# An earlier chain of end columns, earlier border loads, and a split of the weights without masks

## The chip, the core and the metric

The kernel runs on one core of a Trainium2 chip. The core has a matrix engine (PE, with its weight loads shown apart as PEld), a vector engine (DVE), a scalar engine (ACT), a general engine (POOL) and a queue that issues DMA transfers (SP). Each engine takes its instructions in the order of its own queue and waits on semaphores for the others. The metric is the device time of one execution in microseconds (us); for a kernel it is the median of its runs.

## The reference

The program adds two blocks to x, an array of 32 samples by 64 channels by 1024 positions. Each block is a chain of four modulated convolutions followed by a feed-forward part over the 1024 positions as features:

```python
x = x + _L0_ffn_ref(_L0_cond_ref(x, cond_512, ...), L0_ffn_A, L0_ffn_B, L0_ffn_Wr)
x = x + _L1_ffn_ref(_L1_cond_ref(x, cond_512, ...), qweight, scales, zeros, bias)

# _L0_cond_ref and _L1_cond_ref: 4 layers, 'same', 'upsample', 'same', 'downsample'
s = style @ mw.T + mb                          # a scale for each sample and channel
weight = SCALE * w * s[:, None, :, None]       # 64 x 64 x 3 for each sample
weight = weight * rsqrt(sum(weight * weight))  # normalised over input channel and tap
out = conv(x, weight) + b                      # up- and downsampling with a blur (1, 3, 3, 1)

# _L0_ffn_ref: 64 experts of rank 16, the best 16 for each of the 2048 rows
scores = xf @ Wr.T
top_vals, top_idx = top_k(scores, 16)
gates = softmax(top_vals)                      # scattered into G, 2048 x 64
h = einsum('nd,krd->nkr', xf, A)
out = einsum('nkr,kdr->nd', h * G[:, :, None], B) * 2

# _L1_ffn_ref: weights of 4 bits, unpacked
W = scales * q - zeros
out = x @ W + bias
```

All of it is in 32-bit floats. The kernel works on 16 pairs of samples, two samples of 64 channels on the 128 partitions.

## The kernel before

**Stages.** For the first block the kernel goes through the 16 pairs, and for each pair p it does the following, with the parts of neighbouring pairs laced into one another. `begin` prepares the positions. `first` (c, L760 and L761, for later pairs L772 and L777) is the first part of the four convolutions. `composed1` and `composed2` (`compose` and `weights` in the main loop) multiply the last layers' weights of the pair into one another: g at L600, f at L623, the evictions of f by ACT at L638, L640 and L641, and sums by POOL at L646 and L652. `rest` (`later` in the main loop, r at L811 for the first samples, at L838, L856 and L879 for others) is the rest of the convolutions with the composed weights, which leaves the tokens thx of the pair. `layer0` multiplies the tokens with A and Wr (h at L959), picks the gates (L993 to L1003, on DVE), and `gated` (L1009, on POOL) multiplies the gates in; the result goes to memory as hgd. When all pairs are done, the kernel turns h round (ht, L1085), multiplies with B (o, L959 again, in `layer0b`) and adds the residual (L1129 and L1130, on DVE), which gives x1. The second block follows in the same manner, with the unpacked weights (q, L1211).

**Whole and split products.** Pairs 0 and 1 use A and B as they came from memory, in full float (araw and, for part 7 of A, kept; braw, which lies in cv). The other pairs use weights taken apart into a high part, a low part and a crossed part in a shorter float format (fp32r): wa for A, wb for B, each in eight parts k. `split_weights` (L375 to L390) makes them. For each part it goes over chunks of 512 columns (A with Wr has 1088 columns, so two chunks of 512 and one of 64; B has 1024). DVE masks the low bits off (L150, into a small buffer wah or wbh), POOL subtracts the masked from the raw weights (L383), and ACT copies the masked into the high part (L384). Over the whole part, DVE then makes the crossed part (L391) from the two. The tokens are split in the same way, by DVE (L150, L923), ACT (L927, L931) and POOL (tdx and tdh, L939). The raw weights of A lie in blocks which later hold split weights: wa5 takes the block of araw0, wa6 that of araw1, and wa7 that of araw2. wb k takes the block of wa k.

**End columns.** The first and last columns of each sample need their own treatment, since the border of each layer is padded. `ends` is a generator that does this for all 16 pairs at once, as a chain: DVE scales the loaded border columns xg of x (L493, L494); PE makes ye (L502), DVE scales it (L474, L477); PE makes ue (L521), DVE scales and blurs it (L530 to L532); PE makes ve (L546), DVE scales and blurs it; PE makes re (L559), DVE adds the bias; PE turns it round (rt, L568), ACT copies it, and DMAs write it to the array red (L574). From there or from rt the outermost rows come to the tokens, for pairs 0 and 1 by the DMAs of `outer` (L907) and for others by those of `outer_outputs` (L590). Each `next(set_ends)` in the main program advances the chain by one step.

**What sets the order.** The program is written once in one order, and each engine gets its own instructions from it in an order that a scheduler makes by priority. `tc.issue_after(x)` holds an instruction behind x, and only an instruction that runs on the same engine as x. The list `beside` gives what is laced in between the stages of a pair's product: `beside[n]` runs ahead of the n-th `next(main)`. Buffers come from pools: h and o use 4 banks of PSUM (fps), f, g, ue, ve and re share one (mps), and ye and c use 3 (cps).

**Loads of the start.** SP issues x of the first pairs, then A and Wr in four groups (`load_a`, L395 to L415: parts 2 to 4, then 5, 0 and 1, then 6, then 7), and then the border columns xg (L413, two transfers of 64 KB).

Of the kernel before, what the change touches and what calls it, by code (L numbers as in the profile page):

```python
# [8 lines left out]
F32 = mybir.dt.float32  # L9
# [3 lines left out]
ALU = mybir.AluOpType  # L13
AX = mybir.AxisListType

P = 128
# [4 lines left out]
NP = B // 2  # L21
L = 1024
# [3 lines left out]
H = 512  # L26
# [12 lines left out]
AW = E + E * R  # L39
# [24 lines left out]
def adaln_ffn_kernel(ctx: ExitStack, tc: tile.TileContext, t, out: bass.AP):  # L64
    nc = tc.nc
# [46 lines left out]
    re = const.tile([P, 2, 2, P], F32, name="re")  # L112
    xg = const.tile([P, NP, 2, 8], F32, name="xg")
# [29 lines left out]
    def block(k, shape, dt, name):  # L143

        return wts.tile(shape, dt, tag=f"w{k}", name=name)

    def high(src, name):

        v = wk.tile([P, H], I32, tag="hi", name=name, bufs=3)[:, : src.shape[1]]
        nc.vector.tensor_scalar(  # L150
            v, src.bitcast(I32), BITS, BITS, ALU.logical_shift_right, ALU.logical_shift_left
        )
        return v.bitcast(F32)

    done, tbl, outers, uppers = {}, {}, {}, {}
    WHOLE = (0, 1)
# [219 lines left out]
    def split_weights(raw, w, ks, into, name, crossed=True):  # L376

        for k in ks:
            ws = block(k, [P, 3, w], F32R, f"{name}{k}")
            for c in range(0, w, H):  # L380
                cs = slice(c, min(c + H, w))
                h = high(raw[k][:, cs], f"{name}h{k}_{c}")
                nc.gpsimd.tensor_tensor(ws[:, 1, cs], raw[k][:, cs], h, ALU.subtract)  # L383
                nc.scalar.copy(ws[:, 0, cs], h)  # L384
            into[k] = ws
            if crossed:
                crossed_weights(into, k)
# [7 lines left out]
    def load_a():  # L395

        wr = t["wrT"].rearrange("(s q) e -> s q e", q=NC)
        av = t["aT"].rearrange("(s q) f -> s q f", q=NC)
        raw = [None] * NC
        for n, parts in enumerate((((2, 5),), ((5, 6), (0, 2)), ((6, 7),), ((7, 8),))):  # L400
            if n < 3:
                r = block(5 + n, [P, 3, AW], F32, f"araw{n}")
            else:
                r = wk.tile([P, AW], F32, tag="w4", name="kept", bufs=3).unsqueeze(1)
            j = 0
            for a, b in parts:
                nc.sync.dma_start(r[:, j : j + b - a, E:], av[:, a:b])
                nc.sync.dma_start(r[:, j : j + b - a, :E], wr[:, a:b])
                for q in range(a, b):
                    raw[q] = r[:, j + q - a]  # L410
                j += b - a
        for s, c in enumerate((0, L - 8)):
            nc.sync.dma_start(xg[:, :, s], t["x"][:, :, c : c + 8].rearrange("n p w -> p n w"))  # L413
        return raw

    def load_b(ks, into):
# [552 lines left out]
    def layer0(p, ws):  # L969

        hs = wk.tile([P, AW], F32, tag="w4", name=f"hs{p}", bufs=3)
        key = f"x0_{p}"
        whole = p in WHOLE

        def joined(col, w, qd):
            dst = hs[:, col : col + w]
            if whole:
                nc.scalar.activation(dst, qd[0], AF.Copy, scale=alp[:, NL - 1, p : p + 1])
                return
            nc.scalar.activation(dst, qd[0], AF.Copy, scale=outd[:, 0, p : p + 1])  # L980
            nc.vector.scalar_tensor_tensor(
                dst, qd[1], outd[:, 1, p : p + 1], dst, ALU.mult, ALU.add
            )

        ga = tiny.tile([P, E], F32, tag="ga", name=f"ga_{p}")

        def gates():
            s0 = hs[:, :E]
            m0 = tiny.tile([P, 8], F32, tag="m0", name=f"m0_{p}")
            m1 = tiny.tile([P, 8], F32, tag="m1", name=f"m1_{p}")  # L990
            s1 = tiny.tile([P, E], F32, tag="s1", name=f"s1_{p}")
            s2 = tiny.tile([P, E], F32, tag="s2", name=f"s2_{p}")
            nc.vector.max(m0, s0)  # L993
            nc.vector.match_replace(s1, m0, s0, LOW)
            nc.vector.max(m1, s1)
            nc.vector.match_replace(s2, m1, s1, LOW)
            su = tiny.tile([P, 1], F32, tag="su", name=f"su_{p}")
            nc.vector.tensor_scalar_mul(su, m0[:, 0:1], -1.0)
            nc.scalar.activation(ga, s0, AF.Exp, bias=su)
            nc.vector.scalar_tensor_tensor(ga, s2, LOW, ga, ALU.is_equal, ALU.mult)  # L1000
            nc.vector.reduce_sum(su, ga, axis=AX.X)
            nc.vector.reciprocal(su, su)  # L1002
            done["gates"] = nc.vector.tensor_scalar_mul(ga, ga, su)  # L1003

        def gated(c):
            a, b = CHUNKS[c]
            v = hs[:, E + a * R : E + b * R].rearrange("p (e r) -> p e r", r=R)
            g = ga[:, a:b].unsqueeze(2).to_broadcast([P, b - a, R])
            nc.gpsimd.tensor_tensor(v, v, g, ALU.mult)  # L1009

        def chunk(c):
            a, b = CHUNKS[c]
            w = (b - a) * R + (E if c == 0 else 0)
            col = a * R + (E if c > 0 else 0)
            banks = [fpst(f"h{p}_{c}_{j}")[:, :w] for j in range(1 if whole else 2)]
            return banks, slice(col, col + w)

        def done_with(c, ch):
            product(ch, key, ws, at, D)
            joined(ch[1].start, ch[1].stop - ch[1].start, ch[0])  # L1020

        if whole:

            three = [chunk(c) for c in range(3)]
            ks = (2, 3, 4, 5, 0, 1, 6, 7)
            for n, k in enumerate(ks):
                for ch in three:
                    product(ch, key, ws, at, Q, (k,), ks[0], ks[-1])
                if n in (0, 1, 2, 3, 5):
                    yield  # L1030
            for c, ch in enumerate(three):
                done_with(c, ch)
            gates()
            yield
            for c in range(3):
                gated(c)
            nc.sync.dma_start(hgd[p], hs[:, E:])
            return

        two = []  # L1040

        ks = tuple(range(6 if p == len(WHOLE) else NC))
        for c in range(2):
            two.append(chunk(c))
            product(two[c], key, ws, at, Q, ks)
            yield
        for c in range(2):
            if p == len(WHOLE):
                product(two[c], key, ws, at, D, ks)
            else:  # L1050
                done_with(c, two[c])
                if c == 0:
                    gates()
            yield
        if p == len(WHOLE):
            for c in range(2):
                product(two[c], key, ws, at, Q, (6, 7))
                product(two[c], key, ws, at, D, (6, 7))
                joined(two[c][1].start, two[c][1].stop - two[c][1].start, two[c][0])
                if c == 0:  # L1060
                    gates()
        ch = chunk(2)
        product(ch, key, ws, at, Q)
        yield
        done_with(2, ch)
        yield
        for c in range(3):
            gated(c)
        nc.sync.dma_start(hgd[p], hs[:, E:])

    def load_h(p):
# [219 lines left out]
    def weights(k):  # L1291
        if k < len(todo):
            fw[k] = composed2(*todo[k], gs.pop(k))

    def later(k, h):
        if k < len(todo):
            i, p = todo[k]
            rest(i, 2 * p + h, ys[k][h], fw[k][h])
# [10 lines left out]
    def split_behind(v, k):  # L1309
        with tc.issue_after(done[v].ins):  # L1310
            split_weights(araw, AW, (k,), wa, "wa")
# [32 lines left out]
    compose(1)  # L1344
    with tc.issue_after(done["c"].ins):
        split_weights(araw, AW, (3,), wa, "wa")
    for h in range(2):
        later(0, h)
    spread_rows(1)
    weights(1)  # L1350
    load(2)
    tables_of(2)
    set_ends = ends(0, 0, NP, block(2, [P, 3 * AW], F32, "room2"))
    next(set_ends)

    for k in range(NP):
# [6 lines left out]
            hg = load_h(0)  # L1363
        main = layer0(k, araw if k in WHOLE else wa)
        next(main)
        if k == 0:
            split_behind("xe", 0)
            split_behind("xe", 1)
        if k + 3 < NP:
            tables_of(k + 3)  # L1370
            if k + 2 >= DIRECT:
                load(k + 3)
        beside = [[] for _ in range(5)]
        if k == 0:
            beside[0] += [(next, set_ends)]
            beside[1] += [(next, set_ends)]
            beside[2] += [(next, set_ends)]
            beside[3] += [(split_behind, "s2", 4), (run, set_ends), (outer, 0), (outer_of, 2)]
            beside[4] += [(split_behind, "re", 2)]
        if not last:  # L1380
            beside[1] += [(later, k + 1, 0)]
            beside[3] += [(later, k + 1, 1)]
# [27 lines left out]
            with tc.issue_after(done["gates"].ins):  # L1410
                split_weights(araw, AW, (7,), wa, "wa", False)
        run(main)
        if k == 0:
            weights(k + 2)
        if not last:
            crossed(f"x0_{k + 1}")

# [3 lines left out]
    for p in range(NP):  # L1421
# [19 lines left out]
        if p == LAST:  # L1441
            load(NP)
            tables_of(NP)
            set_ends = ends(1, 0, LAST, cv[:, O_FW:])
# [108 lines left out]
```

## Time and profile before

| | us |
|---|---|
| median of 3 runs | 893.77 |
| lowest and highest run | 892.96, 894.99 |
| profiled execution | 891.84 |
| its span | 889.8 |
| outside of the span | 2.0 |

| engine | busy us | share of the span |
|---|---|---|
| PE | 861.4 | 97% |
| PEld | 773.3 | 87% |
| DVE | 723.9 | 81% |
| POOL | 531.8 | 60% |
| ACT | 355.6 | 40% |

The profile is of one execution. An instruction's row gives its start from the beginning of the span, its time, its engine and line, what it writes and reads, and, in brackets, how long its engine was idle before it and which instruction of which engine ended this. Rows of like instructions that follow each other are drawn together (x6). PE's granted clock is 1.00 when it is full. The products of the first block run until about 395 us, those with B until about 640, and the second block's after that.

The borders of the stages that the change touches, from the timeline of PE: the first r of pair 0 begins at 29.85, ye is made at 38.53, ue at 41.17, ve at 49.55, re at 54.43 and rt at 59.60. f of pair 2 begins at 72.56. The first r of pair 2 begins at 79.22. The first products with split weights are at 100.93, the last products with A end at 395.5, and the first products with split B begin at 426.53.

### The profile page before, as it was taken

The numbers are of one execution on the slowest core, as the hardware profiler recorded it, in microseconds if no ns is written. First come the engines' busy times: TensorE is split into PE (matmuls) and PEld (weight loads), VectorE is DVE, ScalarE is ACT, GpSimd is POOL, SyncE is SP. The second block draws the span as 40 slices with busy tenths as digits, with TensorE's granted clock in tenths as the row PEclk, the third lists the DMA queues.
The fourth block names the chain that finished last, engine by engine and source line by source line (L and its number), as shares of the span: only waits on it lengthen the run. The fifth ranks groups of instructions, "written<-read, shape, count | busy, mean of one in ns | idle before, by whom it ended". The sixth has DMA issues, their size and how long they took to land.

```text
span 889.8 us, 14891 instructions
## 1 busy us (share of the span) xinstructions
PE 861.4 (97%) x5023; PEld 773.3 (87%) x5023; DVE 723.9 (81%) x1461; ACT 355.6 (40%) x817; POOL 531.8 (60%) x745
## 2 busy tenths in 40 slices
PE   6989989999999999999999999999999999999997
PEld 5877789999999999994688888888899999999996
DVE  5565888888888888768996666669999999999996
ACT  6444444444444444433432221247333433443340
POOL 7335754666666665556572222343887888888884
PEclk9999999999999999999999999999999999999999
DMA  8531213222222222344465765566433234324311
GB/s 244 147 73 51 52 62 86 83 81 82 78 76 74 74 76 72 119 166 155 140 213 193 229 195 175 189 194 190 146 107 110 87 118 118 110 96 140 107 66 72
DMA packets 49739, 107.83 MB, mean 121 GB/s; under 512 B 13764, under 2 KB 22400, under 8 KB 49664
## 3 DMA queue, kind: packets, MB, share of 16 engines
q1 hardware_dynamic: 48704, 105.90, 37.9%
q10 hardware_dynamic: 960, 0.99, 0.5%
q8 instruction: 40, 0.66, 0.3%
q14 instruction: 35, 0.29, 0.1%
HBM read 69.00 MB, written 37.86 MB: 120 GB/s over the span
## 4 chain that ended last, share of the span: by engine, by line
PE 41%; DVE 8%; POOL 2%; issue 2%; ACT 0%; DVEq 0%; POOLq 0%
PE o L959 16%; PE q L1211 11%; PE f L623 3%; PE r L879 2%; PE c L777 2%; PE r L838 1%; PE ht L1085 1%; PE r L847 1%; PE c L772 1%; PE g L600 1%; DVE cv L720 1%; DVE cv L778 1%; DVE r L888 1%; DVE rt L870 1%; DVE nib L443 1%
## 5 line engine op out<-in xcount | busy, mean ns | idle before, releaser
L720 DVE TENSOR_TENSOR cv<-cv 128x257 f32<-128x257 f32 x120 | 106.7, 921 | 1.1 <-ACT cv L762 0.9
L734 POOL TENSOR_TENSOR cv<-cv 128x256 f32<-128x256 f32 x120 | 77.5, 646 | 28.8 <-DVE cv L720 15.9
L726 POOL TENSOR_TENSOR cv<-cv 128x128 f32<-128x128 f32 x100 | 38.8, 409 | 68.1 <-DVE su L1002 55.1
L1211 PE MATMUL q<-wq,thx 128*128 128x342 f32 x384 | 73.1, 332 | 3.5 <-ACT thx L917 2.9
L1211 PE MATMUL q<-wq,tlx 128*128 128x342 f32 x384 | 72.3, 330 | 0.0
L959 PE MATMUL h<-wa,tdx 128*128 128x352 f32 (+1 forms) x336 | 72.0, 350 | 0.2 <-DVE wa L391 0.2
L623 PE MATMUL f<-gs,iw 128*128 128x128 f32 (+1 forms) x384 | 68.2, 327 | 0.0
L623 PEld LDWEIGHTS f<-gs,iw 128*128 128x128 f32 x384 | 61.9, 191 | 5.5 <-POOL iw L260 0.2
L1211 PEld LDWEIGHTS q<-wq,thx 128*128 128x128 f32 x384 | 60.4, 189 | 5.5 <-ACT thx L917 4.0
L959 PE MATMUL h<-wa,thx 128*128 128x352 f32 (+1 forms) x336 | 64.8, 334 | 0.0
L774 ACT ACTIVATE yt<-c,be,al 128x257 f32<-128x257 f32 x56 | 31.7, 566 | 80.4 <-PE c L772 80.3
L879 PE MATMUL r<-cv 128*128 128x128 f32 x480 | 63.4, 275 | 0.0
L1211 PEld LDWEIGHTS q<-wq,tlx 128*128 128x128 f32 x384 | 61.6, 189 | 0.8
L959 PE MATMUL h<-wa,tlx 128*128 128x352 f32 (+1 forms) x336 | 62.3, 327 | 0.0
L959 PE MATMUL o<-wb,thh 128*128 128x512 f32 x224 | 59.8, 401 | 1.6 <-ACT wb L384 1.6
L939 POOL TENSOR_TENSOR tdx<-thx,tlx 128x1024 fp32r<-128x1024 f32 x14 | 35.4, 2532 | 43.0 <-ACT tlx L931 34.7
L959 PEld LDWEIGHTS h<-wa,tdx 128*128 128x128 f32 x336 | 56.8, 188 | 2.4 <-DVE wa L391 0.5
L879 PEld LDWEIGHTS r<-cv 128*128 128x128 f32 x480 | 58.4, 191 | 0.0
L646 POOL TENSOR_TENSOR cv<-cv 128x256 f32<-128x256 f32 x60 | 50.2, 836 | 13.2 <-ACT cv L641 13.1
L959 PE MATMUL o<-wb,tlh 128*128 128x512 f32 x224 | 58.0, 397 | 0.0
L638 ACT COPY cv<-f 128x256 f32<-128x256 f32 x64 | 23.9, 374 | 85.3 <-PE f L623 71.8
L980 ACT ACTIVATE hs<-h,outd 128x368 f32<-128x368 f32 (+1 forms) x42 | 23.7, 564 | 83.4 <-PE h L959 83.1
(318 smaller groups left out, 2266.9 us busy)
## 6 DMA issues: line engine op xcount, KB each, us to landing
cv<-in_x_dram SPq DMA_DIRECT2D x60, 256.0 KB
cv<-x1e SPq DMA_DIRECT2D x64, 192.5 KB
x1e<-dd SPq DMA_DIRECT2D x16, 514.0 KB
hgd<-hs SPq DMA_DIRECT2D x16, 512.0 KB
hg<-hgd SPq DMA_DIRECT2D x16, 512.0 KB
x1d<-x SPq DMA_DIRECT2D x16, 512.0 KB
xb<-x1d SPq DMA_DIRECT2D x16, 512.0 KB
out_dram<-o SPq DMA_DIRECT2D x15, 512.0 KB
```

The lines of the kernel that those rows point to most:

```text
L623: done["f"] = nc.tensor.matmul(pv[:, n : n + 2 - k], iw[:, e].rearrange("p a b -> p (a b)"), v, start=(m == 0), stop=(m == len(steps) - 1) ...
L638: nc.scalar.copy(f8[:, 0::2], pv[:, :, h])
L646: nc.gpsimd.tensor_tensor(f[:, 4 * P : 6 * P].rearrange("p (a b) -> p a b", b=P), v[:, :, 0], v[:, :, 1], ALU.add,)
L720: nc.vector.tensor_tensor(d[:, k], yo[:, k : k + HQ], yb, ALU.subtract)
L726: nc.gpsimd.tensor_tensor(y[:, YB + k * P : YB + (k + 1) * P], y[:, 2 * k : 2 * k + 2 * P - 1 : 2], y[:, 1 : 2 * P : 2], ALU.subtract,)
L734: nc.gpsimd.tensor_tensor(e[:, :, k], d[:, :, 2 * k : 2 * k + HQ - 2 : 2], d[:, :, 1 : HQ - 1 : 2], ALU.subtract,)
L774: nc.scalar.activation(yt, mid, AF.Identity, bias=be0[:, n : n + 1], scale=a)
L879: done["r"] = nc.tensor.matmul(ps[:, j * P : (j + 1) * P], y[:, YE + (2 * q + k) * P : YE + (2 * q + k + 1) * P], w(q + 2 * k), start=True ...
L939: done["td"] = nc.gpsimd.tensor_tensor(*(v.rearrange("p a b -> p (a b)") for v in (td, *toks[key])), ALU.subtract)
L959: nc.tensor.matmul(banks[l == 2], toks[key][l][:, order(k)], w[:, cols], start=(k == first and l != 1), stop=(k == last and l in (2, min(n ...
L980: nc.scalar.activation(dst, qd[0], AF.Copy, scale=outd[:, 0, p : p + 1])
L1211: nc.tensor.matmul(ps, half[:, k], wq[at(k)][:, c * QC : (c + 1) * QC], start=(k == 0 and j == 0), stop=(k == NC - 1 and j == 1),)
```

## The change

1. `split_weights` no longer masks. ACT copies the raw part into the high part, all columns in one instruction, and POOL subtracts this high part, as it was rounded, from the raw part, also in one instruction. The crossed part is made as before. DVE loses 40 masks, and POOL now needs ACT's copy first. What `issue_after` held back were the masks; without them it holds nothing of the split on ACT and POOL.
2. The two loads of xg stand behind the second group of A's loads, and no longer behind the fourth.
3. For pair 2 `gated` stands behind the sums of a composed weight (L652) on POOL.
4. The chain of end columns begins earlier: ye between the r of pair 0's two samples, ue after the second, ve, re and rt beside the first products of pair 0. The splits of parts 0 and 1 of A follow the chain's third step, that of part 4 comes behind its fourth ("re"), with part 2. `outer(0)` and `outer_of(2)` come earlier, and f of pair 2 (`weights(2)`) stands ahead of the last products of pair 0.

```diff
@@ split_weights
-            for c in range(0, w, H):
-                cs = slice(c, min(c + H, w))
-                h = high(raw[k][:, cs], f"{name}h{k}_{c}")
-                nc.gpsimd.tensor_tensor(ws[:, 1, cs], raw[k][:, cs], h, ALU.subtract)
-                nc.scalar.copy(ws[:, 0, cs], h)
+            nc.scalar.copy(ws[:, 0], raw[k][:, :w])
+            nc.gpsimd.tensor_tensor(
+                ws[:, 1], raw[k][:, :w], ws[:, 0].bitcast(F32), ALU.subtract
+            )
@@ load_a
-        for s, c in enumerate((0, L - 8)):
-            nc.sync.dma_start(xg[:, :, s], t["x"][:, :, c : c + 8].rearrange("n p w -> p n w"))
+            if n == 1:
+                for s, c in enumerate((0, L - 8)):
+                    nc.sync.dma_start(
+                        xg[:, :, s], t["x"][:, :, c : c + 8].rearrange("n p w -> p n w")
+                    )
@@ layer0
         for c in range(3):
-            gated(c)
+            with tc.issue_after(done["sum"].ins) if p == len(WHOLE) else nullcontext():
+                gated(c)
@@ the main program
-    for h in range(2):
-        later(0, h)
+    set_ends = ends(0, 0, NP, block(2, [P, 3 * AW], F32, "room2"))
+    later(0, 0)
+    next(set_ends)
+    later(0, 1)
+    next(set_ends)
     spread_rows(1)
     weights(1)
     load(2)
     tables_of(2)
-    set_ends = ends(0, 0, NP, block(2, [P, 3 * AW], F32, "room2"))
     next(set_ends)
...
-        if k == 0:
-            split_behind("xe", 0)
-            split_behind("xe", 1)
...
         if k == 0:
-            beside[0] += [(next, set_ends)]
-            beside[1] += [(next, set_ends)]
-            beside[2] += [(next, set_ends)]
-            beside[3] += [(split_behind, "s2", 4), (run, set_ends), (outer, 0), (outer_of, 2)]
-            beside[4] += [(split_behind, "re", 2)]
+            beside[0] += [(next, set_ends), (split_behind, "s3", 0), (split_behind, "s3", 1)]
+            beside[1] += [(run, set_ends), (outer, 0), (outer_of, 2)]
+            beside[3] += [(split_behind, "re", 4)]
+            beside[4] += [(split_behind, "re", 2), (weights, 2)]
...
         run(main)
-        if k == 0:
-            weights(k + 2)
```

## The prediction

> **What bounds the kernel now.** I read the page first (shares, slices, chain), then what each wait cost the matrix engine, PE, by stretches of the span, then the timeline around the largest waits on PE, ACT, DVE and POOL.
>
> ```profile
> PE 861.4 (97%) x5023; PEld 773.3 (87%) x5023; DVE 723.9 (81%) x1461; ACT 355.6 (40%) x817; POOL 531.8 (60%) x745
> PE   6989989999999999999999999999999999999997
> ```
>
> PE is busy for 97% of 889.8 us, so an edit of other engines gains only what PE now waits for. The change acts in three places, A (25 to 79 us: ends chain beside the first products), B (80 to 133: last splits of A) and C (393 to 443: splits of B). PE's waits above 0.8 us in them, and two smaller ones (engine, what waited, for what: us in all, times, longest):
>
> ```profile
> PE ve L546 <- DVE room L532: 3.0, 1, 3.0
> PE c L777 <- DVE rt L870: 1.0, 1, 1.0
> PE r L838 <- POOL cv L652: 0.9, 1, 0.9
> PE re L559 <- DVE room L532: 0.6, 1, 0.6
> PE c L777 <- DVE tlx L923: 0.6, 1, 0.6
> ...
> PE r L838 <- POOL cv L652: 1.5, 1, 1.5
> ...
> PE o L959 <- ACT wb L384: 1.6, 2, 0.9
> ```
>
> Together 9.2 us: A holds 3.0 + 0.6 + the 0.9, B 1.0 + 0.6 + 1.5, C 1.6. In C the waits cost more than their length (PE's timeline: start, us, instruction, idle before; then PE's row of two windows, granted clock before the DMA share):
>
> ```profile
> 430.32 0.80 PE L959 MATMUL o<-wb,thh 128*128 128x512 f32 x1 [0.91 <-ACT wb L384]
> 430.92 3.32 PE L959 MATMUL o<-wb,tlh 128*128 128x512 f32 x8
> 434.07 1.98 PE L959 MATMUL o<-wb,thh 128*128 128x512 f32 x8
> ```
> ```profile
> 431.00:432.00 1.00, 1.00 (x4) 0.81 (x3) 1.00 (x2) 0.94 (x4) 1.00 (x1) 0.50 0.95 385
> ```
>
> The eight tlh took 3.32 at a granted clock of 0.50 against 1.98 for the same eight at 435.88. The o products that began at 426.53 would have reached 434.07's place at 426.53 + 2 x 1.93 = 430.4, so C loses 3.7 in all. The 3.0 us wait at 46.5 cost its length alone: the clock there reads 1.00.
>
> **A: the ends chain earlier.** No PE work is removed; ye, ue, ve, re and rt stand between r of pair 0 and the first h products, and f of pair 2 (weights(2)) comes before the last h instead of after. PE, walked with before's durations: r_0 ends 31.9, rows .58; ye needs thx (DVE .69) and L493/L494 (.25 each, pipelined), so it starts at 33.15 after a wait of about 0.7, the only new one. This asks that xg has landed by 32.6: its two loads, 5.5 us of issuing on SP, move from 22.06 ahead to 15.9, and A's parts 6 and 7 go back by the same 5.5 on SP's queue; they are first read past 65. The row table's store and the next loads of x, behind all of these in both orders, keep their places. Then r_1 3.85, ue .74, h .65, f_1 2.0, 4 h 2.44: 43.65. ve needs the blur (DVE L530-L532, 1.2 us, done 40.6) and the bank of f_1, whose six evictions on ACT end 43.55: no wait. ve 1.1, h, r_2 (6), re, r_2 (2), rt, r_2 (8), h, c_4, g_2, h: 56.3. r_3 3.85, h x2 3.65, f_2 2.0, c_5 1.7, h x2 3.7, h x2 3.7: r_4 at 75.0, before 79.22. The outer rows that h k0 needs have landed by 55, needed at 60; f_2's POOL sums are done by 69, so the 0.88 goes. Terms: -3.0 -0.65 -0.88 -0.2 (rows L355's wait) + 0.7 = **-4.0**, walked -4.2; I take -4.2, ends -3.3 (ye waits 1.6) and -4.5 (no wait).
>
> **B: the ACT queue.** The three masks of the last part (DVE 106.85, 1.96) go, and with them the 1.02 on rt L870 (behind them on DVE's queue), the 0.17 on wa L391 and most of the 0.64. gated behind the sums of f_4 lets POOL do L646/L652 before the 1.83 of L1009: the 1.51 goes; the store of hgd behind it is read far later, past 395. That is -3.2. But the mask was also what held the ACT copy back: issue_after orders DVE's mask alone. Without it the copy of part 7 takes its place in ACT's queue by priority, ahead of the three evictions L978 of pair 1's h, and it must wait, because wa7 takes the block of araw2, which the POOL subtract of wa6 still reads:
>
> ```profile
> 100.24 0.73 POOL L652 TENSOR_TENSOR cv<-cv 128x256 f32<-128x256 f32 x1
> 100.93 3.52 POOL L383 TENSOR_TENSOR wa<-araw,wah 128x512 fp32r<-128x512 f32 x3
> ```
> ```profile
> 100.59 1.01 ACT L978 ACTIVATE hs<-h,alp 128x352 f32<-128x352 f32 x2
> ```
> ```profile
> 103.14 1.16 PE L959 MATMUL h<-wa,thx 128*128 128x368 f32 x6
> ```
>
> Chain: the subtract begins at 100.93 (L646, L652 of f_3 and tdx stand before it in both orders), one instruction of 1088 columns, 2.5 to 3.1 (L939, 1024 columns: 2.35 to 2.59; the split by chunks 3.52): 103.7. ACT copy 1.1 (L931, 1024 columns, 1.06): 104.8, L978 .56: 105.4. The h at 103.14 takes the bank which that eviction frees: a new wait of 2.3 (2.2 to 3.0), and behind the copy in ACT's queue all three L978 and so DVE's gates. Sum **-0.8**, ends -1.6 (wait 1.6, the shift of A helping POOL) and +1.0 (DVE's gates late too). If a wait of this size drops the clock as in C (1.34 plus the edges), +1.7 more.
>
> **C: split of B.** 16 masks go (0.68 alone, .89 mean) and the two waits with their 3.7. In exchange ACT copy, POOL subtract and DVE L391 form a chain per k, and POOL's eight long subtracts bound it. Nearest rows:
>
> ```profile
> 402.32 2.29 DVE L391 SCALAR_TENSOR_TENSOR wb<-wb 128x1024 fp32r<-128x1024 f32 x1
> ```
> ```profile
> 403.49 2.25 POOL L383 TENSOR_TENSOR wb<-cv,wbh 128x512 fp32r<-128x512 f32 x1
> ```
>
> L391 alone takes 1.22 (405.77), the 512 subtract alone 1.27; side by side 2.29 and 2.25: nearly one after the other. So a k costs 2.35 + 1.0 = 3.4; bounds 2.35 (no loss) and 4.5 (twice the worst chunk). From 395 with one gated (1.0) before it wb7 ends near 423, its L391 near 424.5. On DVE the residual sum x_0 (L1130, 411.2 before) now stands behind L391 of wb0 to wb5 and its second half behind wb7's: 424 to 426. Behind it in DVE's queue wait hh and tlh of pair 2 (PE asks for thh at 426.5: +0.8); on SP the store of x_0 and behind it the load of the next residual (issue 427, landing 432); on ACT the DMA of cw (behind L1173), hence DVE L213 to L216, then x_1 at 438.8, whose bank PE wants at 437.2 (+1.3); further +0.5 at ht of pair 1. That leaves -1.1 for PE, but DVE, with x_1 so late, reaches L1129 (the evictions whose banks the next pair takes, 441.94 before) only at 443.0, and the last 1.1 goes there: **0**. Ends -2.5 (pace 3.0, a few tenths of waits) and +2.0.
>
> [...]
>
> After 443 the order of all engines is the same and PE-bound: gains pass through.
>
> **Sum.** -4.2 -0.8 +0 = -5.0 against the profiled execution's own 891.84 (span 889.8 and 2.0 around it): 886.8. That execution is 1.93 below the median of the runs shown, 893.77; on the median 888.8. What a measurement can tell from no change is 0.2%, 1.8 us.
>
> **Rivals.**
> - *C keeps its gain* (POOL pace 2.4, DVE's chain early): -4.2 -0.8 -3.7 = 885.1. For it: POOL lost only 1.0 beside L391. Against: DVE's queue puts x_0 behind wb5 whatever the pace.
> - *B eats A's gain*: new wait 3.0 instead of 2.3 with the clock loss of 1.7, and C +0.6: -4.2 + 1.6 + 0.6 = 891.8, the edge of same. For it: in C a clock fell after waits; against: 3.0 us at 46.5 did not.
> - *xg lands late*: ye waits until 36.6 as before, A gains 0.9 for f_2's sums alone: 892.1. Against: SP issues it 6 us earlier.
> - *Slower: POOL's subtracts in C run at their worst rate throughout.* Pace 4.5: wb7 and x_0 come 8 x 1.1 = 8.8 later, and so do thh of pair 2 and x_1; PE waits all of it: -5.0 + 8.8 = 897.6. It decides above a pace of 3.4 + 5.0/8 = 4.0, and is slower by over 0.2% above 4.25. For it: one chunk took 2.25 and one L391 3.40. Against: those were single ones, medians 1.45 and 2.04.
>
> **How the numbers follow.** Forecast case 0.44 (own range 886.6 to 891.2), C keeps its gain 0.17, B eats it 0.13, xg late 0.06, slower 0.20. Faster: 0.44 + 0.17 + half of the two middle cases less a tail of 0.05: 0.65; same 0.15; slower 0.20. The range runs from 884.8 (C's gain nearly whole) to 895.0 (half way into the slow case, to leave no more than 2 in 10 out).
>
> **What would show it.** Right: no wait at ve above 0.3, one of 0.5 to 0.9 at ye L502; first r of pair 2 at 74.5 to 75.5; one wait of 2.2 to 3.0 at the third h of pair 1, released by ACT L978; no wait on wb from ACT; in C L381 of 1024 columns at 2.4 to 3.4 and x_0's second half past 422. Wrong: ye released by DMA past 34; L391 and L381 side by side at over 4 us a k; a granted clock of 0.5 near 105; PE waiting for thh over 2 us at about 425.

## The result and the profile after

The change made the kernel slower: 900.4 us in the median (896.83 to 903.98, 7 runs) against 894.25 (892.58 to 895.42, 7 runs), a ratio of 1.0072 with a 95% interval of 1.0048 to 1.0096. Forecast were 888.8 and a range that ended at 895.0. The profiled execution of the changed kernel took 901.68, its span is 899.9; that of the kernel before took 891.84 with a span of 889.8, so the two traces differ by 10.1 where the medians differ by 6.2. Line numbers of the changed kernel are up to 3 higher than before's.

The page of the changed kernel (engines' busy time, then the granted clock of PE in 40 slices):

```profile
PE 867.9 (96%) x5023; PEld 779.0 (87%) x5023; DVE 713.4 (79%) x1421; ACT 351.4 (39%) x793; POOL 528.0 (59%) x721
PEclk9799999999999999999899999999999999999999
```

DVE has 40 instructions and 10.5 us less to do, but PE is *longer* busy with the same 5023 matrix products: they ran at half speed for longer at the start (a pair of c in 1.06, later in 0.60), and the clock was not fully granted in the second slice (0.7 in the row) and again in the middle (0.8). PE's waits in the first 130 us, and then the largest between 395 and 645:

```profile
PE h L961 <- ACT hs L980: 2.2, 1, 2.2
PE cs L337 <- DVE room L340: 2.1, 1, 2.1
...
PE ye L504 <- DVE room L496: 0.6, 1, 0.6
...
PE o L961 <- DVE x L1133: 6.6, 1, 6.6
```

The waits that the prediction meant to remove are gone: none at ve, re, the first r of pair 2, rt, nor for ACT's copies of wb. Three new ones of size stand in their place: the 2.2 at h and the 6.6 at o, which the prediction had (the second as 1.3), and the 2.1 at cs, which it had not. The 0.6 at ye was forecast at 0.7.

Where the time went, by the start of the same PE instruction in both traces:

| PE reaches | before | after | difference | in this stretch |
|---|---|---|---|---|
| f of pair 0 | 18.48 | 21.17 | +2.7 | +2.7 |
| r of pair 0, after g of pair 1 | 29.85 | 37.00 | +7.2 | +4.5 |
| first r of pair 2 | 79.22 | 84.52 | +5.3 | -1.9 |
| first o with B | 397.40 | 401.32 | +3.9 | -1.4 |
| first o with wb | 426.53 | 430.70 | +4.2 | +0.3 |
| ht after pair 2's o | 442.14 | 451.35 | +9.2 | +5.0 |
| end of the span | 889.8 | 899.9 | +10.1 | +0.9 |

The first 2.7 are no part of the change. The chain to it runs 0.5 later, and PE's first matrix products run at half speed for longer: a pair of c takes 1.06 until about 20 us in this execution and until about 13.5 in that of before, then 0.60 (the clock row reads 1.00 all the time). Both lengths occur with one and the same kernel: the kernel of the experiments e8 and e12 below had f of pair 0 at 18.66 in one profiled execution and at 21.08 in the other. The last 0.9 hold a wait of 1.3 for DVE at c L779, which was 0.3 before; it is 1.3 in e1 and e10 too, and 0.3 in e9, which differ in neither split, so it is not put down to the change.

**The start.** The rows of DVE, POOL and PE of the changed kernel there:

```profile
27.83 2.50 DVE L340 TENSOR_TENSOR room<-room 128x32 f32<-128x32 f32 x1
```
```profile
27.81 2.47 POOL L381 TENSOR_TENSOR wa<-araw,wa 128x1088 fp32r<-128x1088 f32 x1 [8.10 <-DMA xg<-in_x_dram]
```
```profile
30.39 1.39 PE L337 MATMUL cs<-room,cw 128*128 128x32 f32 x6 [2.08 <-DVE room L340]
```
```profile
32.00:34.00 2.00, 2.00 (x9) 1.52 (x8) 1.21 (x2) 0.20 (x1) 0.00 (x0) 0.50 0.00 0
38.00:40.00 2.00, 2.00 (x12) 2.00 (x11) 0.00 (x0) 0.04 (x1) 0.00 (x0) 0.50 0.72 150
```

The kernel before, DVE and POOL:

```profile
25.37 0.19 DVE L340 TENSOR_TENSOR room<-room 128x32 f32<-128x32 f32 x1
```
```profile
25.59 2.94 POOL L383 TENSOR_TENSOR wa<-araw,wah 128x512 fp32r<-128x512 f32 x3 [6.41 <-DVE room L340]
```

L340 adds two arrays of 128x32. Before, it took 0.19, and POOL's first chunk began only when it had ended: the masks stood around L340 in DVE's queue. In the changed kernel it begins 0.02 behind POOL's subtract of part 3 of A, now one instruction of 1088 columns, and ends 0.05 behind it. cs waits 2.1 for it, and behind this wait PE's clock stands at 0.50 (the number ahead of the last two of a window's row) from 31 to 41.

**C.** The rows of DVE, SP, ACT's queue and PE of the changed kernel, from the residual sum of pair 0 to D of pair 2:

```profile
405.91 16.55 DVE L390 SCALAR_TENSOR_TENSOR wb<-wb 128x1024 fp32r<-128x1024 f32 x5 [2.26 <-POOL wb L381]
422.38 1.06 DVE L1133 SCALAR_TENSOR_TENSOR x<-o,xres 128x512 f32<-128x512 f32 x1
423.28 3.61 DVE L390 SCALAR_TENSOR_TENSOR wb<-wb 128x1024 fp32r<-128x1024 f32 x2
426.81 1.04 DVE L1133 SCALAR_TENSOR_TENSOR x<-o,xres 128x512 f32<-128x512 f32 x1
...
437.13 1.09 DVE L1133 SCALAR_TENSOR_TENSOR x<-o,xres 128x512 f32<-128x512 f32 x1 [5.64 <-DMA cv<-in_mw_dram]
443.81 0.96 DVE L213 TENSOR_TENSOR cv<-cv 128x768 f32<-128x768 f32 x1 [5.58 <-DMA cv<-in_cw_dram]
...
446.00 1.03 DVE L1133 SCALAR_TENSOR_TENSOR x<-o,xres 128x512 f32<-128x512 f32 x1
```
```profile
430.28 0.74 SPq L1114 DMA_DIRECT2D xres<-in_x_dram  x1
```
```profile
438.33 0.47 ACTq L200 DMA_DIRECT2D cv<-in_cw_dram  x1
```
```profile
447.09 3.62 PE L961 MATMUL o<-wb,tdh 128*128 128x512 f32 x8 [6.62 <-DVE x L1133]
```

The sum of pair 0 before, both halves:

```profile
411.20 1.96 DVE L1130 SCALAR_TENSOR_TENSOR x<-o,xres 128x512 f32<-128x512 f32 x2
```

The chain: crossed parts, the sum of pair 0 (422.4 and 426.8), its stores on SP, the load of the next residual behind them (issued at 430.28), the first half of pair 1's sum at 437.13, the load of cw on ACT's queue behind that, L213 when it lands at 443.8, and then the second half of pair 1's sum, whose bank PE wants. DVE waits twice by 5.6 for a load. The row at 437.13 names the load of mw, which the sum does not read; mw was issued right behind the residual, and of what the sum reads only the residual was still being loaded, so that it waited for the residual is inferred. PE's clock falls again during the 6.6 (it reads 0.50 from 443.5 to 450.4): eight tdh take 3.62.

### The profile page after: what moved, and what is told of

Read it like the earlier page. It is cut to its first block, busy times and chain, and to the rows that moved or that the text cites. A ratio compares the mean times of both kernels' runs of the same rounds, so it can differ in the third digit from the quotient of the medians.

```text
span 899.9 us, 14776 instructions
## 1 busy us (share of the span) xinstructions
PE 867.9 (96%) x5023; PEld 779.0 (87%) x5023; DVE 713.4 (79%) x1421; ACT 351.4 (39%) x793; POOL 528.0 (59%) x721
## 5 line engine op out<-in xcount | busy, mean ns | idle before, releaser
L722 DVE TENSOR_TENSOR cv<-cv 128x257 f32<-128x257 f32 x120 | 109.1, 940 | 0.9 <-ACT cv L764 0.8
L961 PE MATMUL o<-wb,tdh 128*128 128x512 f32 x224 | 56.6, 402 | 6.7 <-DVE x L1133 6.6
L961 PEld LDWEIGHTS h<-wa,thx 128*128 128x128 f32 x336 | 54.9, 189 | 2.8 <-ACT hs L980 2.5
```

Of the source, the lines that this page charges most:

```text
L722: nc.vector.tensor_tensor(d[:, k], yo[:, k : k + HQ], yb, ALU.subtract)
L961: nc.tensor.matmul(banks[l == 2], toks[key][l][:, order(k)], w[:, cols], start=(k == first and l != 1), stop=(k == last and l in (2, min(n ...
```

## The experiments

The ratios are to the kernel before, each measured beside its own runs of it; 0.1% is 0.9 us. The changed kernel itself stands at 1.0072.

| kernel | median us | ratio | 95% interval |
|---|---|---|---|
| e1, masks kept, all else of the change | 887.83 | 0.9926 | 0.9907 to 0.9944 |
| e2, split without masks alone | 903.69 | 1.0099 | 1.0081 to 1.0116 |
| e3, part 3 of A later | 894.81 | 1.0003 | 0.9986 to 1.0021 |
| e4, masks for B only | 895.75 | 1.0014 | 0.9995 to 1.0033 |
| e5, B's crossed parts later | 892.06 | 0.9961 | 0.9947 to 0.9976 |
| e6, part 7 of A behind the evictions | 899.47 | 1.0049 | 1.0035 to 1.0064 |
| e7, part 3's subtract in chunks | 896.74 | 1.0033 | 1.0018 to 1.0048 |
| e8, e1 with B as in e5 | 886.19 | 0.9899 | 0.9883 to 0.9915 |
| e9, e1 with xg loaded late | 888.88 | 0.9939 | 0.9919 to 0.9959 |
| e10, e1 with gated early | 889.85 | 0.9952 | 0.9933 to 0.9971 |
| e11, e3 + e5 + e6 | 882.52 | 0.9871 | 0.9853 to 0.9888 |
| e12, e8 again | 886.12 | 0.9901 | 0.9882 to 0.9920 |

### Which part of the change costs the time (e1, e2)

e1 takes the changed kernel and puts the old split back:

```diff
-            nc.scalar.copy(ws[:, 0], raw[k][:, :w])
-            nc.gpsimd.tensor_tensor(
-                ws[:, 1], raw[k][:, :w], ws[:, 0].bitcast(F32), ALU.subtract
-            )
+            for c in range(0, w, H):
+                cs = slice(c, min(c + H, w))
+                h = high(raw[k][:, cs], f"{name}h{k}_{c}")
+                nc.gpsimd.tensor_tensor(ws[:, 1, cs], raw[k][:, cs], h, ALU.subtract)
+                nc.scalar.copy(ws[:, 0, cs], h)
```

> The changed kernel with the old split by masks; the earlier ends chain, the earlier loads of xg and the later gated stay. Theory (the split without masks costs the time, in the start and in C; the ends chain gains what its walk said): L340 takes 0.2 us again, the first r begins near 30, the first r of pair 2 near 75.0, the wait of 1.51 at pair 2's f stays away; sum -4.2 - 1.5 against before, about 888.5. Rival (the earlier loads of xg disturb the start, the split has no part in it): the first r stays near 37 and the time at 893 or more.

e2 is the reverse of this diff on the kernel before.

> The kernel before with the split without masks alone. Theory: both losses are there without the other parts: L340 is held some 2.5 us beside POOL's long subtract, PE's clock falls to 0.5 behind that wait, and D of pair 2 waits about 6 for the residual sum; +6.8 in the start, +5.3 in C, less about 1.2 for the masks' wait in B: 903 to 906. Rival (the losses come from the new order of the start): 892 to 895.

Measured: e1 887.83, e2 903.69, both as the theory had them. In e1 L340 took 0.19 at 25.75, and the first r of pair 2 came at 75.61 (the prediction's walk: 75.0). In e2 the three new waits are there without any of the change's other parts:

```profile
PE h L958 <- ACT hs L977: 2.2, 1, 2.2
PE cs L337 <- DVE room L340: 2.1, 1, 2.1
```

and 6.5 at o for the residual sum. The ends chain with its companions is worth -0.74%, some 6.6 us; the split without masks, as it is placed here, costs more than that.

### The start (e3, e7)

e3 holds ACT's copy of part 3 behind the copy of the row table on ACT, which itself comes after L340 and L343. (The `done["c"]` that stood there is a product on PE, so it held none of the split's instructions, in the kernel before either.)

```diff
-        nc.scalar.copy(rows, ps[:B, :C])
+        done["rows"] = nc.scalar.copy(rows, ps[:B, :C])
...
-    with tc.issue_after(done["c"].ins):
+    with tc.issue_after(done["rows"].ins):
         split_weights(araw, AW, (3,), wa, "wa")
```

> The changed kernel with the ACT copy of part 3 of A held behind the copy of the row table (L356) on ACT, so that POOL's subtract begins after DVE's L340 and L343 are done. Theory (L340, an operation of 128x32, was locked out by the subtract of 1088 columns, and PE's wait for it dropped the clock): L340 back to 0.2, no wait at cs, clock 1.00 from 30 to 42, about 6.8 less than the changed kernel: 893 to 894. Rival (L340 was slow for another reason, or the clock falls there anyway): 899 to 901.

e7 leaves the subtract where it is and cuts it up:

```diff
+            for c in range(0, w, H if k == 3 and name == "wa" else w):
+                cs = slice(c, min(c + (H if k == 3 and name == "wa" else w), w))
                 nc.gpsimd.tensor_tensor(
-                    ws[:, 1], raw[k][:, :w], ws[:, 0].bitcast(F32), ALU.subtract
+                    ws[:, 1, cs], raw[k][:, cs], ws[:, 0, cs].bitcast(F32), ALU.subtract
                 )
```

> The changed kernel with POOL's subtract for part 3 of A in chunks of 512, 512 and 64 columns behind the same single ACT copy. Theory (DVE's operation with two inputs in SBUF is locked out until the one POOL instruction that runs ends): L340 takes about 1.2 instead of 2.5, PE's wait at cs 0.8 instead of 2.1; if the clock then stays up, 894 to 895, if it falls all the same, about 899. Rival (L340 waits for the whole subtract or for another thing): 2.5 as before and 900.

Rows of DVE and POOL in e3, where the two no longer meet, and then of DVE, POOL and PE in e7:

```profile
27.30 0.19 DVE L340 TENSOR_TENSOR room<-room 128x32 f32<-128x32 f32 x1
```
```profile
30.48 2.49 POOL L381 TENSOR_TENSOR wa<-araw,wa 128x1088 fp32r<-128x1088 f32 x1 [11.14 <-DMA araw<-in_aT_dram]
```
```profile
25.45 1.30 DVE L340 TENSOR_TENSOR room<-room 128x32 f32<-128x32 f32 x1
```
```profile
25.43 2.77 POOL L383 TENSOR_TENSOR wa<-araw,wa 128x512 fp32r<-128x512 f32 x3 [5.97 <-ACT wa L380]
```
```profile
26.80 0.85 PE L337 MATMUL cs<-room,cw 128*128 128x32 f32 x6 [0.87 <-DVE room L340]
```

L340 took 0.19 without the subtract, 1.30 with chunks of 512 columns (1.27 is what such a chunk took in the kernel before) and 2.50 with one of 1088. In the changed kernel it ended at 30.33, with the one subtract (30.28), and in e7 at 26.75, about when the first of the three chunks was done (25.43 plus the 1.27 of such a chunk), while the three ran until 28.20. So in these traces it waits for the POOL instruction that runs, whole, and no longer than that one.

The clock stayed at 1.00 in both kernels from 28 to 44. From f of pair 0 to ye PE takes 21.5 in the changed kernel, 14.8 in e3 and 15.7 in e7: 6.7 and 5.7 less. By the ratios e3 gains 0.69% on the changed kernel, 6.2 us, and e7 0.39%, 3.5 us, which the two intervals only just let reach 5.7. Part of the gap lies in the clock elsewhere. In the traces of e3 and e7 (and of e2 and e5) it falls behind the 2.2 at h as well, where it stayed up in the changed kernel's. The tlx behind that wait in the changed kernel and in e3, and e3's window:

```profile
111.78 1.16 PE L961 MATMUL h<-wa,tlx 128*128 128x368 f32 x6
```
```profile
104.59 1.74 PE L961 MATMUL h<-wa,tlx 128*128 128x368 f32 x6
```
```profile
105.00:107.00 2.00, 2.00 (x10) 2.00 (x9) 1.90 (x4) 0.00 (x0) 1.32 (x1) 0.50 0.00 0
```

From the first split product of A to the first o this costs 1.4 in e3 and 1.3 in e5 and e7. In e7's trace another 1.3 goes near the end, where the clock is down from 882 to 886 (the mean granted clock of that execution is 0.990). Which waits end in half clock differs from trace to trace (the 2.2 at h does in four of the six that have it), so a ratio of medians holds more than the edit.

### C (e4, e5)

e4 is the changed kernel with the masked split where the name is wb. e5 keeps B without masks and moves the crossed parts on DVE:

```diff
-            nc.vector.scalar_tensor_tensor(
+            done["x1"] = nc.vector.scalar_tensor_tensor(
                 x4[:, c * P : (c + 1) * P],
...
-            split_weights(braw, L, range(4 * p, 4 * p + 4), wb, "wb")
+            split_weights(braw, L, range(4 * p, 4 * p + 4), wb, "wb", False)
+            if p == 1:
+                with tc.issue_after(done["lo"].ins):
+                    for k in range(4, NC):
+                        crossed_weights(wb, k)
...
         run(main)
+        if p == 0:
+            with tc.issue_after(done["x1"].ins):
+                for k in range(4):
+                    crossed_weights(wb, k)
```

> The changed kernel with the old masked split for B alone. Theory (in C the split without masks puts the residual sums x of pairs 0 and 1 behind the crossed parts on DVE, and the loads behind the stores of x land too late for pair 2): the wait of 6.6 at D of pair 2 goes, the two waits for ACT's wb copy of 0.7 and 0.9 and their half clock come back; -5.3 against the changed kernel, about 895. Rival (the loads land late for another reason, as the shift of the start): the wait stays above 4 and the time at 899 or more.

> The changed kernel with B's crossed parts 0 to 3 held behind the residual sum of pair 0 and parts 4 to 7 behind the low tokens of pair 2 on DVE; the split itself stays without masks. Theory (in C the harm is DVE's order, with the residual sum behind six and eight crossed parts, and the loads that hang on it; not the split): the sum of pair 0 is done by 420 again, the wait of 6.6 goes, and no wait for ACT's copies comes in its place; 890.5 to 892.5, which is 3 to 5 under the changed kernel with masks for B. Rival (POOL's long subtracts hold DVE up whatever its order): a wait above 3 at D of pair 2, 896 or more.

Measured: e4 895.75, 0.58% or 5.2 us under the changed kernel; e5 892.06, 1.11% or 9.9 under it. DVE and PE in e5:

```profile
415.83 1.08 DVE L1133 SCALAR_TENSOR_TENSOR x<-o,xres 128x512 f32<-128x512 f32 x1 [5.81 <-PE o L961]
...
429.58 1.08 DVE L1133 SCALAR_TENSOR_TENSOR x<-o,xres 128x512 f32<-128x512 f32 x1
430.49 3.51 DVE L390 SCALAR_TENSOR_TENSOR wb<-wb 128x1024 fp32r<-128x1024 f32 x2
433.92 0.94 DVE L213 TENSOR_TENSOR cv<-cv 128x768 f32<-128x768 f32 x1
434.79 1.10 DVE L1133 SCALAR_TENSOR_TENSOR x<-o,xres 128x512 f32<-128x512 f32 x1
```
```profile
438.42 3.80 PE L961 MATMUL o<-wb,tdh 128*128 128x512 f32 x16
```

Pair 0's sum now waits for PE alone, pair 1's second half is done at 435.9, before PE begins the tdh at 438.42, and the sixteen run without a wait. So the harm in C was DVE's order and the chain of loads behind it, not the split. The mended order beats the masks by 0.53% (e4's trace has the waits of 0.7 and 0.9 for ACT's copies again, and 1.1 at the next pair, which e5 lacks). POOL's seven subtracts took 17.25 in e5, 2.46 each, with one crossed part of DVE beside them, and 22.15 in the changed kernel, 3.16 each, with five and parts of two more; the first one, with no crossed part beside it, took 2.37 in both. In these two traces the pace goes with how many crossed parts DVE runs beside them.

### B (e6)

```diff
-                nc.scalar.activation(dst, qd[0], AF.Copy, scale=alp[:, NL - 1, p : p + 1])
+                done["joined"] = nc.scalar.activation(
+                    dst, qd[0], AF.Copy, scale=alp[:, NL - 1, p : p + 1]
+                )
...
-            with tc.issue_after(done["gates"].ins):
+            with tc.issue_after(done["joined"].ins):
                 split_weights(araw, AW, (7,), wa, "wa", False)
```

> The changed kernel with ACT's copy of part 7 of A held behind the three evictions of pair 1's h. Theory: the wait of 2.2 at the third h goes and nothing late comes in its place, since part 7 is read ten us later: about 898.2. Rival (POOL is what is late there, and the subtract of part 7 with its crossed part comes too late for the first D): a wait of 1 to 2 at h with the crossed part, and 900.

PE's waits of e6 in the first 130 us:

```profile
PE c L779 <- DVE tlx L925: 0.6, 1, 0.6
...
PE r L840 <- DVE cv L780: 0.5, 1, 0.5
...
PE h L961 <- DVE wa L390: 0.2, 1, 0.2
```

The 2.2 is gone, and 1.3 of smaller waits, which the 2.2 had covered but for 0.2, come out behind it: from the first split product of A to the first o e6 gains 0.8 on the changed kernel's trace, and 2.0 to 2.1 on those of e3, e5 and e7, where the clock fell behind the 2.2. The ratios say 2.1, with intervals that overlap. The theory had the wait's cause right and what is late next wrong.

### The parts of the gain (e9, e10), and better versions (e8, e11, e12)

e9 issues xg after the fourth group of loads again (`if n == 3`); e10 calls gated without `issue_after`. Both start from e1.

> The kernel of the first experiment (ends chain, later gated, masks kept) with the two loads of xg back behind A's last parts. Theory (the loads were early enough before: issued by 27.6, and ye is made near 33.5): ye waits under 1.5, and the time stays within 1.8 of the first experiment's 887.8. Rival (the earlier loads are what lets the chain start early): ye waits 3 or more, the time 890 to 892.

> The kernel of the first experiment with gated of pair 2 where it was before the change. Theory: the wait of 1.5 for the sum at L652 comes back in front of the first r beside pair 2, and nothing else: about 889.3. Rival (POOL is early enough there once the start is earlier): 887.8 and no such wait.

In e9 the time is 1.1 us over e1's, with intervals that overlap, and ye waits 0.6 as in e1: the border columns were early enough where they stood. A wait of 0.5 at ve for an eviction by ACT is new there; whether the late loads bring it was not tested. SP spends 8.9 on issuing them early and 5.56 late, which is why the early place brings them out only 3 us sooner. In e10 the wait is back,

```profile
PE r L841 <- POOL cv L655: 1.5, 1, 1.5
```

and the time is 2.0 over e1's.

e8 is e1 with B split as in e5; e12 is e8 once more, beside e11, which is the changed kernel with the edits of e3, e5 and e6.

> The ends chain, xg and gated as changed, A split with masks as before, B split without masks with its crossed parts held behind the residual sum and the low tokens. Theory: the gain of the ends chain alone (887.8) and in C the two waits for ACT's copies with their half clock gone, 3.7, and the wait of 1.1 at the next pair too: 883 to 885. Rival (some other chain of C is late next): 887 to 888.

> The changed kernel with the three orders mended at once: the copy of part 3 of A behind the row table, that of part 7 behind the evictions, B's crossed parts behind the residual sum and the low tokens. Theory (the split without masks costs nothing but these three collisions): 900.4 - 5.6 - 8.3 - 0.9 = 885.6, level with the best so far. Rival (POOL's long subtracts cost DVE something elsewhere too): 888 or more.

> The best so far once more (A split with masks, B without, with the crossed parts held behind), as the measure for the run beside it: 885.5 to 887.

e8 came out at 886.19 and 886.12, over the forecast 883 to 885, with an interval that overlaps e1's. e11 is the fastest, 882.52, 1.29% under the kernel before (0.9871, 0.9853 to 0.9888), and 3.6 under e12 on the same chip, with intervals that overlap by little, where level was expected. Its page:

```profile
PE 858.7 (98%) x5023; PEld 772.3 (88%) x5023; DVE 700.9 (80%) x1421; ACT 351.5 (40%) x793; POOL 524.4 (60%) x721
```

Against the changed kernel the three edits give 18.0 us together (2.01%), and 18.2 one by one (0.69%, 1.11% and 0.23%); the forecast 885.6 had added the differences of the medians, 14.8. The spans of e11 and e12 differ by 5.8 (880.5 and 886.3). Of these 2.3 are the long ramp at the start of e12's profiled execution, and 1.6 lie between the first q and the end, where its clock was down from 873 to 877 (the mean granted clock is 0.998 in e12's execution, 0.999 in e11's). Another 1.6 lie between the first split product of A and the first o (294.4 in e11, 295.9 in e8 and e12), where e8 and e12 still wait 1.0 at c for DVE's rt. That part alone looks like the edit's; the 3.6 between the medians is not shown to be.

## Why the prediction was wrong

**The step that failed first was not in the working at all.** The walk of A began at r of pair 0, "r_0 ends 31.9", with the start as before. But part 3 of A is split in the start, between L340 and L343, on which cs and through it everything waits. The section on C weighed how POOL's long subtract and DVE's L391 slow each other, and held it for a loss of 1.0 a part; that a DVE operation of 0.19 could be held up for the whole of a POOL instruction, on a path that ends at PE, was asked nowhere. It cost 4.5 to r_0 and 2.3 more to ye, of half clock, where the sum had no term. e3 takes it away (6.2 by the ratios) and e7 halves the wait.

**A was right.** From ye to the first r of pair 2 the walk had 75.0 - 33.15 = 41.85, and the trace has 84.52 - 42.63 = 41.89. The one new wait, at ye, was forecast at 0.7 and is 0.60; none at ve, as said. With an undisturbed start (e1) ye is at 33.71 and the first r of pair 2 at 75.61. The earlier xg, which the prediction wrote into A's condition, is worth nothing that was measured (e9), and its two loads held SP for 8.85 and not 5.5.

**B was right in its mechanism and size.** The new wait at the third h, released by ACT L980, was forecast at 2.3 and is 2.18. The stretch gave -1.4 in this execution, forecast -0.8 with ends -1.6 and +1.0. That the clock stayed up here was luck: behind the same wait it fell in four of six traces (e2, e3, e5, e7; not in the changed kernel's and e4's). In e3, e5 and e7 the stretch then gains nothing against before (318.0 to 318.2 from the first r of pair 2 to the first o; before 318.2). The prediction had named this fall, at 1.7, as a case beside its sum; it measures 1.3 to 1.4. The 1.51 removed by the later gated comes back in e10.

**C had the chain right and one term of it too small.** POOL's pace was 3.16 a part (3.4 forecast) and the residual sum of pair 0 ended at 427.85 (424 to 426 in before's time, which is 4 earlier here, so it was early). The load of the next residual went out when it was forecast to, at 430.28, 426.1 in before's time (427). But pair 1's first half came at 433.0 in that time instead of 432, and cw, issued behind it, landed 5.4 later, so that the second half of the sum ended at 442.9 instead of 438.8. The wait was 6.6 where 1.3 was forecast, and in it the clock fell, which the forecast for C had left out. C cost 5.3 from the first o with B to ht, forecast 0 with ends -2.5 and +2.0. The rival that was to end slower named this queue and the place, but as its price the pace of POOL, which in fact was fast.

**The 3.7 that C was to win holds for one execution.** From the first o with split B to ht PE takes 15.6 in before's trace and 11.8 in e5, e8, e11 and e12, which have neither wait: 3.8. But the half clock behind the two waits for ACT's copies does not come with them each time. In e1, e4, e9 and e10 the same two waits, 0.73 and 0.91, are followed by eight tlh in 2.1, and the stretch takes 14.1, so there only 2.3 is to be won. Here e1, PE:

```profile
425.02 0.50 PE L962 MATMUL o<-wb,thh 128*128 128x512 f32 x1 [0.91 <-ACT wb L384]
425.35 2.09 PE L962 MATMUL o<-wb,tlh 128*128 128x512 f32 x8
```

In sum, in the two traces: -4.2 in A was met, -0.8 in B came as -1.4, 0 in C became +5.3, and +6.8 in the start was not seen. That makes 6.5; with the 2.7 ahead of the change and the last 0.9 it is the 10.1 between the spans. Three figures of the prediction do not follow from its own rows, and none of them decides: x_1 at 438.8 against 437.2 is a wait of 1.6, not 1.3; B's terms add up to about -0.9; and a mask of B alone takes 0.4, not 0.68.

## What to carry to other kernels

An edit that merges short POOL instructions into long ones can lengthen a DVE operation that happens to start beside them, however small it is (L340, 128x32, went from 0.19 to 2.50 here); look for such operations on the path to PE in every place where the merged instruction will run, the start included, and put it behind them. A wait that a removed operation carried (here the masks, which were all that the ordering held back) has to be given to the instructions that remain. When a queue's order moves a sum, follow its stores and the loads that stand behind them by their own landing times, before a pace is argued over.

## What was not expected of the hardware

- A DVE addition of 128x32 took 2.50, 1.30 and 0.19 us beside a POOL instruction of 1088 columns, of 512, and of none.
- PE's clock fell to 0.50 for about 10 us at a wait of 2.1 that had 0.4 of idle time and 1.6 of work ahead of it, in all five traces that have this wait (the changed kernel, e2, e4, e5 and e6). At the wait of 2.2 at h it fell for about 3.5 us in four of six traces. At 0.73 and 0.91 it fell in one of five, and at 3.0 (before, at ve) and 0.9 (e7, at cs) not at all, in one trace each. In these traces the length of a wait alone does not tell, and one and the same wait does not always bring it.
- The half speed at the start lasts until about 13.5 or until about 19 to 20 us, in executions of one kernel (e8 and e12), worth about 2.4 us at f of pair 0.
- Two transfers with runs of 32 bytes held SP for 5.5 us when issued behind all of A (before, e9) and 8.8 to 8.9 when issued behind its second group (the changed kernel, e1).
